# A list scheduler's cost table, replaced by measured instruction spacings, in a Mamba and attention kernel

## The chip, the cores and the metric

The kernel runs on one core of a Trainium2 chip. The metric is the device time of one execution in microseconds (us). A core has five engines that work side by side, each through its own queue in order: PE (TensorE, matrix products), DVE (VectorE), ACT (ScalarE, which also loads a function table when the kind of function changes), POOL (GpSimd) and SP, which here issues the DMA transfers.

## The reference

Two layers are applied to an image batch x of shape (2, 256, 64, 64), float32; each image is 256 channels by 4096 positions.

```python
# layer 0: Mamba, along the 4096 positions of each image
y = group_norm(x);  yn = layer_norm(y) * gamma + beta
xm, z = split(yn @ W_in.T)                      # 512 channels each
u = silu(conv1d(xm, conv_w, 4 taps) + conv_b)
dt, B, C = split(u @ W_xp.T)                    # 16, 16, 16
dt = softplus(dt @ W_dt.T + b_dt)
h[t] = exp(dt[t] * A) * h[t-1] + (dt[t] * u[t]) * B[t]    # state 512 x 16
ym = (sum_n h[t] * C[t] + u * D) * silu(z)
y2 = ym @ W_out.T + yn
x = x + gelu(y2 @ W1.T + b1) @ W2.T + b2 + y2
# layer 1: attention with 8 heads of 32 channels over the 4096 positions
q, k, v = qkv_w @ group_norm(x) + qkv_b
x = x + softmax(q^T k / sqrt(32)) v
```

## The kernel before

The program has two stages, one after the other: `mamba_stage` and `attention`.

**Tiles and steps.** The Mamba stage goes through 16 tiles: 2 images of 8 tiles, each of 512 positions. A tile has four blocks of 128 channels (KD = 4), and the 16 states of each channel are laid out so that four of them share the 128 partitions with 32 channels. This gives 32 steps per tile (STEPS), 512 in all. One step (`step`, from L809) does, for two rows of 128 x 512:

- two decays `da = exp(dt * A)` on ACT (L828)
- one matmul on PE that spreads a row of B over the partitions into `bn`, in PSUM (L444 with `pick`)
- two products `dbu = dtu * B`: one on DVE into `bn` (L834), and one that is on POOL in three steps of four and on DVE in the fourth (also L834)
- two scans on DVE (L839), which are the recurrence along the positions
- a copy of the last state on ACT (L842), `keep`, needed by the next tile
- the product of h with C on POOL, in place, 128 x 1024 (L845), which therefore waits for `keep`
- after every second step, four matmuls on PE that add up over the states into `y` (L871); with the last of a block, DVE multiplies y with the gate z (L881)

**Around the steps.** `front` prepares a tile before its steps start: normalisation, the projection and convolution of each block (`conv`, with SiLU), and `softplus`, whose three POOL products of 128 x 512 are L614, L615 and L617. `gate` makes silu(z). `back` comes after the steps of a tile: W_out (L641), the residual sum (L652), the up-projection with GELU (L666), the down-projection (L675, L677), the final sum (L687) and statistics (L688). `qkv` makes the first image's q, k and v for the attention while the second image's tiles run, so that the second half of the stage has this on top. It evacuates each block on ACT (L730) and DVE (L734) and stores it by DMA (L739, L759). `back` and `qkv` take turns with one buffer `hid` of 8 x 512. dt and dtu go through DRAM: stored at L608, and loaded again in the layout of the steps at L792; rows of B and C are loaded at L804.

**What sets the order.** The order of the Mamba stage isn't written by hand. Each piece of work is added to a `Plan` by `add(engine, due, cost, emit, reads, writes, tables, lands)`: the engine, a due time counted in steps, a cost in us, and what it reads and writes. `Plan.order` then plays the program through once, when the kernel is built: whenever an engine is free, it takes from the ready tasks the one that is due first. A task that needs another function table on ACT ranks SWITCH = 6 steps later, and none more than HORIZON = 24 steps past the oldest open one is taken. The engine is then held for the task's cost (1.3 us more for a table load), and what depends on it counts as ready 0.2 us after its end (HANDOVER), plus `lands` for a DMA. Buffers come from rings with a fixed number of places, and a task without a place waits. The result is one order of instructions for each engine, fixed in the program. On the chip, an engine works through its queue in that order, whatever the planned times were. Costs thus take no time themselves. They only shape the order, and with it the places of the table loads.

The attention stage is emitted in a hand-made order after it: per 128 keys the logits on PE (L1131), exponentials on ACT (L1144), values on PE (L1161), and sums on DVE (L1153, L1191) and POOL (L1185 to L1194).

Of the kernel before, what the change touches and what calls it, by code (L numbers as in the profile page):

```python
# [13 lines left out]
AF = mybir.ActivationFunctionType  # L14
# [5 lines left out]
P = 128  # L20
# [238 lines left out]
def mamba_stage(ctx, tc, xs, stats_out, consts, w, outs, scratch):  # L259
# [13 lines left out]
    nc = tc.nc  # L273
    ident, gmat, lnmat, eps_t = consts
    IMAGES = len(xs)
# [213 lines left out]
    def front(i):  # L489
# [12 lines left out]
        for k in range(KC):  # L502
            add("ACT", due - 41, 0.75, lambda k=k: norm(k), [yn[k], scales_buf[b * KC + k]], [yn[k]])


        mean = Buf(mm)
        add("PE", due - 40, 1.8, lambda: matmul(mean.tile, [(lnmat, yn.tile[:, k, :]) for k in range(KC)]), [yn], [mean])
        sq = [Buf(r_tmp) for _ in range(KC)]
        var = Buf(mm)
        for k in range(KC):  # L510

            def centre(k=k):
                nc.vector.tensor_sub(yn.tile[:, k, :], yn.tile[:, k, :], mean.tile)

            add("DVE", due - 39, 0.7, centre, [mean], [yn[k]])
            square = lambda k=k: nc.scalar.activation(sq[k].tile, yn.tile[:, k, :], AF.Square)
            add("ACT", due - 38, 0.65, square, [yn[k]], [sq[k], var] if k == 0 else [sq[k]])

# [4 lines left out]

        add("PE", due - 37, 1.9, lambda: matmul(var.tile, [(lnmat, s.tile) for s in sq]), sq, [var])
        add("ACT", due - 36, 1.25, rstd, [], [var], ("exp",))
        for k in range(KC):

            def scale(k=k):
                y = yn.tile[:, k, :]
                nc.vector.scalar_tensor_tensor(y, y, gamma[:, k : k + 1], var.tile, ALU.mult, ALU.mult)  # L530

            def shift(k=k):
                y = yn.tile[:, k, :]
                nc.scalar.activation(y, y, AF.Identity, bias=beta[:, k : k + 1])  # L534

            add("DVE", due - 35, 0.75, scale, [var], [yn[k]])
            add("ACT", due - 34, 0.75, shift, [], [yn[k]])
        d.u = [Buf(r_u) for _ in range(KD)]
# [17 lines left out]

        add("PE", due - 14, 3.6, project, d.u, [pp, proj, bc])
        add("ACT", due - 13, 0.6, lambda: nc.scalar.copy(proj.tile[:NP, :], pp.tile[:NP, :]), [pp], [proj])
        add("ACT", due - 13, 0.6, lambda: nc.scalar.copy(bc.tile, pp.tile[:NP, :]), [pp], [bc])
        add("SP", due - 12, 0.4, store_bc, [bc], [d.bc], lands=1.6)  # L560
        add("DVE", due - 12, 0.7, halves, [pp, proj], [proj])
        d.dt, d.dtu = [None] * KD, [None] * KD
# [3 lines left out]
    def conv(d, b, k, due):  # L566

        px, pc, xm = Buf(mm), Buf(mm), Buf(r_xm, 2)
        h = halo_buf[b * KD + k]

        def project():
            matmul(px.tile, [(w_in[:, c, bass.ts(k, P)], d.yn.tile[:, c, :]) for c in range(KC)])

        def convolve():
            matmul(pc.tile, [(taps[:, k, j, :], xm.tile[:, j : j + T]) for j in range(TAPS)])

        def silu():
            nc.scalar.activation(d.u[k].tile, pc.tile, AF.Silu, bias=conv_b[:, k : k + 1])

        add("PE", due, 1.8, project, [d.yn], [px, xm])  # L580
        add("POOL", due, 0.2, lambda: nc.gpsimd.tensor_copy(xm.tile[:, 0:HALO], halo[:, b, k, :]), [h], [xm[0]])
        add("ACT", due + 1, 0.6, lambda: nc.scalar.copy(xm.tile[:, HALO:], px.tile), [px], [xm[1]])
        add("POOL", due + 2, 0.2, lambda: nc.gpsimd.tensor_copy(halo[:, b, k, :], xm.tile[:, T:]), [xm], [h])
        add("PE", due + 2, 3.6, convolve, [xm], [pc, d.u[k]])
        add("ACT", due + 4, 0.6, silu, [pc], [d.u[k]], ("silu",))

    def softplus(d, k, due):
# [21 lines left out]

        add("PE", due, 0.8, lambda: matmul(pd.tile, [(w_dt[:, i, bass.ts(k, P)], d.proj.tile) for i in range(2)]), [d.proj], [pd, dt, lw])  # L610
        add("ACT", due + 1, 1.95, exps, [], [pd, dt], ("exp",))
        add("ACT", due + 1, 1.2, logs, [pd], [lw, w1], ("exp",))
        add("DVE", due + 2, 0.7, rest, [pd], [w1])
        add("POOL", due + 3, 1.27, lambda: nc.gpsimd.tensor_sub(lw.tile, lw.tile, w1.tile), [w1], [lw])  # L614
        add("POOL", due + 3, 1.27, lambda: nc.gpsimd.tensor_add(dt.tile, dt.tile, lw.tile), [lw], [dt])  # L615
        add("SP", due + 3.5, 0.9, lambda: store(d.dt[k], dt, "dt_dram"), [dt], [d.dt[k]], lands=2.0)
        add("POOL", due + 3.5, 1.27, lambda: nc.gpsimd.tensor_mul(lw.tile, dt.tile, d.u[k].tile), [dt, d.u[k]], [lw])  # L617
        add("SP", due + 4, 0.9, lambda: store(d.dtu[k], lw, "dtu_dram"), [lw], [d.dtu[k]], lands=2.0)

    def gate(d, k, due):  # L620

        pz, z = Buf(mm), Buf(r_z)
        d.z.append(z)

        def project():
            matmul(pz.tile, [(w_in[:, c, bass.ds(DI + k * P, P)], d.yn.tile[:, c, :]) for c in range(KC)])

        add("PE", due, 1.8, project, [d.yn], [pz, z])
        add("ACT", due + 1, 0.6, lambda: nc.scalar.activation(z.tile, pz.tile, AF.Silu), [pz], [z], ("silu",))

    def back(i):
# [5 lines left out]
        for m in range(KC):  # L637
# [7 lines left out]
            for k in range(0, KD, 2):  # L645
                reads = d.z if k == 0 else d.z[k : k + 2]
                add("PE", due + 2 * m, 1.9, lambda k=k, project=project: (project(k), project(k + 1)), reads, [po])
            add(
                "DVE",
                due + 2 * m + 1,  # L650
                0.7,
                lambda m=m, po=po: nc.vector.tensor_add(yn.tile[:, m, :], yn.tile[:, m, :], po.tile),  # L652
# [6 lines left out]
        for f in range(KH):  # L659
# [7 lines left out]

            add("PE", due + 5 + 1.5 * f, 1.9, up, [yn], [ph, hid if f == 0 else hid[f]])
            add("ACT", due + 6 + 1.5 * f, 0.7, gelu, [ph], [hid[f]], ("gelu",))
        for m in range(KC):  # L670
# [10 lines left out]
            for f in range(0, KH, 2):  # L681
                reads = [hid, yn[m]] if f == 0 else [hid[f], hid[f + 1]]
                add("PE", due + 19 + 4 * m + f / 2, 2.7 if f == 0 else 1.8, lambda f=f, down=down: down(f), reads, [acc])

# [4 lines left out]

            add("DVE", due + 24 + 4 * m, 1.45, end, [acc], [xt[m], stats_bufs[IMAGES + b][m * NT + t]])  # L690
        store = lambda: nc.sync.dma_start(image_tile(outs[b], t), xt.tile)
        add("SP", due + 29, 1.7, store, [xt], [stored[b * NT + t]], lands=3.3)

    def qkv(b, t, due):
# [25 lines left out]
        for k in range(KC):  # L720
            add("ACT", due + 2, 0.75, lambda k=k: norm(k), [hid[3 + k], scales_buf[(IMAGES + b) * KC + k]], [hid[3 + k]])
        for n, (i, m) in enumerate(((1, 0), (1, 1), (0, 0), (0, 1))):
# [20 lines left out]
            at = due + 3 + 2.2 * n  # L743
            add("PE", at, 1.8, project, [hid[k] for k in range(5)], [pm, *halves])
            add("ACT", at + 0.5, 0.7, high, [pm], [hid[5]])
            add("DVE", at + 1, 0.7, low, [pm, hid[5]], [hid[6]])
            add("SP", at + 1.5, 1.7, store, halves, [], lands=3.3)
        for j in range(0, T // P, 2):
# [15 lines left out]
            at = due + 4 + 2.2 * j  # L764
            add("PE", at, 1.8, project, [hid[k] for k in range(5)], [pv, hid[7]])
            add("ACT", at + 0.5, 0.7, lambda pv=pv: nc.scalar.copy(hid.tile[:, 7, :], pv.tile), [pv], [hid[7]])
            add("SP", at + 1, 1.0, store, [hid[7]], [], lands=2.5)
# [41 lines left out]
    def step(g):  # L809
# [37 lines left out]
        for j in range(2):  # L847
            add("ACT", g - 6 + j, 0.71, lambda j=j: decay(j), [dt[j]], [da[j]], ("exp",))
        add("PE", g - 6, 0.4, broadcast_b, [d.proj], [bn])
        if pooled(g):  # L850
            add("POOL", g - 6, 1.27, lambda: times_b(nc.gpsimd, dbu1, 1, rows_b), [dtu[1], rows_b], [dbu1])
        else:
            add("DVE", g, 0.7, lambda: times_b(nc.vector, dbu1, 1, bn), [dtu[1], bn], [dbu1])
        add("DVE", g, 0.7, lambda: times_b(nc.vector, bn, 0, bn), [dtu[0]], [bn])
        for j, dbu in ((1, dbu1), (0, bn)):
            add("DVE", g, 1.27, lambda j=j: scan(j), [da[j], dbu, state_buf[states[j]]], [h[j]])
        add("ACT", g - 6, 0.25, keep, [h], [state_buf[at] for at in states])
        add("POOL", g - 4, 2.36, times_c, [rows_c], [h])
        if quarter == 0:
# [18 lines left out]

        add("PE", g - 3, 1.9 if qd == 0 else 1.1, add_up, [s.h for s in pair] + ([d.u[k]] if qd == 0 else []), [y])
        if qd == NQ - 1:  # L880
            add("DVE", g + 2.5, 0.7, lambda: nc.vector.tensor_mul(d.z[k].tile, y.tile, d.z[k].tile), [y], [d.z[k]])  # L881

# [578 lines left out]
```

## Time and profile before

| what | value |
|---|---|
| median of 3 runs | 4506.31 us (4498.84 to 4507.30) |
| profiled execution: span from first to last instruction | 4505.2 us |
| granted TensorE clock, mean | 0.977 |
| busy over the span: PE, DVE, ACT, POOL | 94%, 86%, 84%, 85% |
| last y x z product of the Mamba stage (L881) | 2066.8 us after the start |
| first logits of the attention (L1131) | 2115.5 us |
| ACT table loads at L244 | 332, of 1283 ns each |

The page doesn't list a time of its own for the profiled execution; its span is 1.1 us below the median of the runs.

Durations of the instructions that matter below, as means: C product on POOL (L845) 2371 ns, dbu on POOL (L834) 1283, the scans (L839) 1273 and 1264, bn on DVE (L834) 681, decay (L828) 701, state copy (L842) 189, bn matmul 595, GELU (L666) 686. The C products and the dbu products on POOL have 512 and 384 instructions.

How to read it: in a row of the timeline stand the start, the duration, the engine and line, and in brackets how long the engine had been idle before and which instruction ended that. In a table by stretch, each engine has its busy time and in brackets the number of instructions. Instructions that follow each other closely on one engine overlap a little, so that the sum of their durations is more than the time they occupy together. The spacing, from one start to the next, is the smaller number.

### The profile page before, as it was taken

To read this page: it belongs to the slowest core of one execution; us is meant where nothing else is said; L and a number is where in the kernel's file an instruction comes from. 1 tells how busy PE (TensorE), PEld (TensorE's weight loads), DVE (VectorE), ACT (ScalarE), POOL (GpSimd) and SP (SyncE) were. 2 spreads that over 40 slices of the span, in tenths; PEclk is the share of its full clock that TensorE was granted. 3 is DMA by queue.
4 is the path that set the end of the run, shared out by engine and by line. 5 is a ranking of instruction groups with operands and counts; after the bars stand their busy time and mean duration, and the time that the engine had idled before them with its cause. 6 is when DMAs were issued, how large, how long until landed. Compare 5 with 4: busy or idle time off the path is not lost.

```text
span 4505.2 us, 53942 instructions
## 1 busy us (share of the span) xinstructions
PE 4257.1 (94%) x18530; PEld 1642.2 (36%) x18530; DVE 3890.9 (86%) x3309; ACT 3768.4 (84%) x4842; POOL 3807.4 (85%) x2249
## 2 busy tenths in 40 slices
PE   5789999999999999988999999999999999999998
PEld 2233333333333333333333333333353333333333
DVE  4999999999999989894888888888848888888888
ACT  4788888888788889873999999999849999999997
POOL 2999999999999999994788888888728888888886
PEclk8899999999999999999999999999999999999999
DMA  5233333333443434445210140101091110401100
GB/s 192 94 120 101 110 125 122 127 127 127 143 148 134 139 126 140 147 153 144 58 27 17 29 101 17 26 17 30 24 265 35 46 26 17 101 17 29 27 19 8
DMA packets 172281, 389.23 MB, mean 86 GB/s; under 512 B 23392, under 2 KB 49760, under 8 KB 163808
## 3 DMA queue, kind: packets, MB, share of 16 engines
q1 hardware_dynamic: 171120, 383.37, 27.4%
q8 instruction: 147, 2.41, 0.2%
q10 hardware_dynamic: 880, 2.36, 0.2%
q14 instruction: 134, 1.10, 0.1%
HBM read 292.33 MB, written 93.32 MB: 86 GB/s over the span
## 4 chain that ended last, share of the span: by engine, by line
PE 57%; DVE 4%; ACT 3%; POOL 3%; issue 2%; DMA 1%; DVEq 0%; POOLq 0%; SPq 0%; ACTq 0%
PE s L1131 25%; PE po L1161 24%; PE mm L444 3%; DVE h L839 2%; POOL h L845 2%; ACT da L828 1%; ACT L244 1%; PE mm L677 1%; PE s L1016 1%; PE y L871 1%; POOL dbu L834 1%; PE sums_ps L1212 1%; DVE bn L834 1%; PE mm L641 0%; PE bn L444 0%
## 5 line engine op out<-in xcount | busy, mean ns | idle before, releaser
L1153 DVE TENSOR_REDUCE chunk<-chunk 128x1024 f32<-128x4096 f32 x288 | 1270.6, 4412 | 242.4 <-ACT chunk L1144 242.3
L1194 POOL TENSOR_TENSOR acc_p<-acc_p,e 128x1024 f32<-128x1024 f32 x480 | 1151.9, 2400 | 196.7 <-ACT e L1144 178.0
L1144 ACT ACTIVATE chunk<-s 128x1024 f32<-128x1024 f32 x992 | 1121.5, 1131 | 185.5 <-PE s L1131 139.9
L845 POOL TENSOR_TENSOR h<-h,c 128x1024 f32<-128x1024 f32 x512 | 1208.5, 2371 | 42.0 <-ACT state L842 28.9
L1131 PE MATMUL s<-q,k 128*128 128x512 f32 x4096 | 1228.4, 422 | 5.8 <-ACT chunk L1144 4.9
L1161 PE MATMUL po<-chunk,v 128*32 128x512 f32 x3968 | 1121.7, 642 | 0.0
L1161 PE MATMUL po<-e,v 128*32 128x512 f32 x4224 | 1080.0, 605 | 0.0
L1144 ACT ACTIVATE e<-s 128x1024 f32<-128x1024 f32 x1056 | 1072.7, 1019 | 7.4 <-PE s L1131 6.9
L1131 PEld LDWEIGHTS s<-q,k 128*128 128x128 f32 x4096 | 691.3, 188 | 1014.4 <-issue 915.0
L828 ACT ACTIVATE da<-dt_rep,neg_a 128x512 f32<-128x512 f32 x1024 | 690.5, 701 | 128.7 <-DVE h L839 106.0
L1192 POOL TENSOR_TENSOR acc_p<-acc_p,e 128x512 f32<-128x512 f32 x480 | 620.2, 1292 | 129.3 <-ACT e L1144 106.6
L839 DVE TENSOR_TENSOR_SCAN h<-da,state,dbu 128x512 f32<-128x512 f32 x512 | 650.5, 1273 | 42.8 <-POOL dbu L834 40.2
L839 DVE TENSOR_TENSOR_SCAN h<-da,state,bn 128x512 f32<-128x512 f32 x512 | 647.1, 1264 | 11.6
L834 POOL TENSOR_TENSOR dbu<-dtu_rep,b 128x512 f32<-128x512 f32 x384 | 488.5, 1283 | 19.7 <-DMA dtu_rep<-dtu_dram 15.0
L244 ACT ACT_TABLE_LOAD x332 | 426.0, 1283 | 6.7 <-PEq L1451 0.7
L444 PE MATMUL bn<-proj,pick 112*128 112x512 f32 x512 | 296.4, 595 | 112.2 <-DVE h L839 111.6
L871 PE MATMUL y<-h,sum 128*32 128x512 f32 x2048 | 359.1, 635 | 42.2 <-POOL h L845 42.1
L834 DVE TENSOR_TENSOR bn<-dtu_rep,bn 128x512 f32<-128x512 f32 x512 | 348.6, 681 | 41.4 <-PE bn L444 27.8
L1191 DVE TENSOR_TENSOR acc<-acc,e 128x512 f32<-128x512 f32 x448 | 310.7, 694 | 30.9 <-ACT e L1144 17.5
L1161 PEld LDWEIGHTS po<-chunk,v 128*32 128x32 f32 x3968 | 144.3, 108 | 361.5 <-issue 349.9
L444 PE MATMUL mm<-yn,w_in 128*128 128x512 f32 x512 | 254.7, 625 | 10.3 <-ACT yn L534 9.1
L444 PE MATMUL mm<-yn,w 128*128 128x512 f32 x512 | 246.5, 611 | 4.2 <-ACT hid L666 2.1
(143 smaller groups left out, 4016.3 us busy)
## 6 DMA issues: line engine op xcount, KB each, us to landing
dt_rep<-dt_dram SPq DMA_DIRECT2D x128, 512.0 KB, 5.1
dtu_rep<-dtu_dram SPq DMA_DIRECT2D x128, 512.0 KB, 5.7
k<-qk_dram SPq DMA_DIRECT2D x62, 512.0 KB, 7.3
q<-qk_dram SPq DMA_DIRECT2D x124, 256.0 KB, 4.7
b<-bc_dram SPq DMA_DIRECT2D x64, 256.0 KB, 3.0
c<-bc_dram SPq DMA_DIRECT2D x64, 256.0 KB, 3.7
dt_dram<-dt SPq DMA_DIRECT2D x64, 256.0 KB, 2.0
dtu_dram<-lw SPq DMA_DIRECT2D x64, 256.0 KB, 2.3
```

The source lines that it names most:

```text
L244: self.nc.scalar.preload_act_table_set(self.TABLES[task.table])
L444: nc.tensor.matmul(out, lhsT=lhsT, rhs=rhs, start=(i == 0), stop=(i == len(pairs) - 1))
L828: nc.scalar.activation(da[j].tile, dt.tile[:, j, :], AF.Exp, scale=scale)
L834: engine.tensor_mul(out.tile, dtu.tile[:, j, :], rows.tile)
L839: nc.vector.tensor_tensor_scan(h.tile[:, j, :], da[j].tile, dbu.tile, initial, ALU.mult, ALU.add)
L845: nc.gpsimd.tensor_tensor(h.tile, h.tile, rows_c.tile.unsqueeze(1).to_broadcast([P, 2, T]), ALU.mult)
L1131: nc.tensor.matmul(ps[:, j, :], lhsT=keys[i // NT, kt][:, h, kj : kj + P], rhs=queries[i][:, h, :], start=True, stop=True)
L1144: nc.scalar.activation(e, todo[s].s[half], AF.Exp, scale=SCALE)
L1153: nc.vector.tensor_reduce(out, terms, AX.XY, ALU.add)
L1161: nc.tensor.matmul(tiles[i].po[h * D : (h + 1) * D, :], lhsT=v[:, c, g * P + h * D : g * P + (h + 1) * D], rhs=todo[s].e[h // 2][:, h % 2, :],
L1192: nc.gpsimd.tensor_add(acc_p[:, 1, :], acc_p[:, 1, :], eb[:, 1, :])
L1194: nc.gpsimd.tensor_add(acc_p, acc_p, eb)
```

## The change

Only the third argument of `add`, the cost, is changed, in the functions of the Mamba stage. Costs of SP's tasks, of some tiny ones, the due times, the landings, HANDOVER, TABLE, SWITCH, HORIZON and the rings stay. The core of the diff (each line pair cut to its cost):

```diff
# front
-norm 0.75   mean, var (PE) 1.8, 1.9    centre 0.7   square 0.65   rstd 1.25   scale, shift 0.75, 0.75
+norm 0.72   mean, var (PE) 1.72, 1.72  centre 0.6   square 0.52   rstd 1.19   scale, shift 0.66, 0.62
-project (PE) 3.6    proj and bc copies (ACT) 0.6, 0.6     halves (DVE) 0.7
+project (PE) 3.44   proj and bc copies (ACT) 0.48, 0.48   halves (DVE) 0.72
# conv
-add("PE", due, 1.8, project, [d.yn], [px, xm])
+add("PE", due, 1.72, project, [d.yn], [px, xm])
-xm copy (ACT) 0.6    convolve (PE) 3.6    silu (ACT) 0.6
+xm copy (ACT) 0.49   convolve (PE) 3.44   silu (ACT) 0.59
# softplus
-PE 0.8   exps 1.95   logs 1.2    rest (DVE) 0.7    three POOL products 1.27 each
+PE 0.5   exps 1.76   logs 0.97   rest (DVE) 0.58   three POOL products 1.23 each
# gate
-PE 1.8    silu 0.6
+PE 1.72   silu 0.5
# back
-W_out pair 1.9    sum (DVE) 0.7   up 1.9    gelu 0.7    down 2.7, then 1.8     end (DVE) 1.45
+W_out pair 1.72   sum (DVE) 0.6   up 1.72   gelu 0.59   down 2.58, then 1.72   end (DVE) 1.37
# qkv
-norm 0.75   project 1.8    high (ACT) 0.7    low (DVE) 0.7    v project 1.8    v copy (ACT) 0.7
+norm 0.71   project 1.72   high (ACT) 0.59   low (DVE) 0.66   v project 1.72   v copy (ACT) 0.49
# step
-            add("ACT", g - 6 + j, 0.71, lambda j=j: decay(j), [dt[j]], [da[j]], ("exp",))
-        add("PE", g - 6, 0.4, broadcast_b, [d.proj], [bn])
+            add("ACT", g - 6 + j, 0.63, lambda j=j: decay(j), [dt[j]], [da[j]], ("exp",))
+        add("PE", g - 6, 0.26, broadcast_b, [d.proj], [bn])
-dbu on POOL 1.27   dbu and bn on DVE 0.7, 0.7
+dbu on POOL 1.23   dbu and bn on DVE 0.6, 0.6
-            add("DVE", g, 1.27, lambda j=j: scan(j), [da[j], dbu, state_buf[states[j]]], [h[j]])
-        add("ACT", g - 6, 0.25, keep, [h], [state_buf[at] for at in states])
-        add("POOL", g - 4, 2.36, times_c, [rows_c], [h])
+            add("DVE", g, 1.185, lambda j=j: scan(j), [da[j], dbu, state_buf[states[j]]], [h[j]])
+        add("ACT", g - 6, 0.1, keep, [h], [state_buf[at] for at in states])
+        add("POOL", g - 4, 2.32, times_c, [rows_c], [h])
-add_up (PE) 1.9 with the block's first, else 1.1    y times z (DVE) 0.7
+add_up (PE) 1.92 with the block's first, else 1.06   y times z (DVE) 0.58
```

The program that comes out has the same arithmetic and the same instructions in another order on every engine, save for the table loads on ACT, which follow the order.

## The prediction

> **What bounds the kernel now.** First the page's engine shares and the rows by slice; the first half of the span is the Mamba stage, the second the attention, whose order is written out by hand and which the change does not touch.
>
> ```profile
> PE 4257.1 (94%) x18530; PEld 1642.2 (36%) x18530; DVE 3890.9 (86%) x3309; ACT 3768.4 (84%) x4842; POOL 3807.4 (85%) x2249
> ...
> DVE  4999999999999989894888888888848888888888
> ACT  4788888888788889873999999999849999999997
> POOL 2999999999999999994788888888728888888886
> ```
>
> The averages mislead: in the Mamba slices POOL is at 9 throughout, which its 85% of the whole span hides. So next the busy times by stretch. I cut at 106 us (POOL is running the steps), at 1180 (the second image's tiles, with the first image's QKV work beside them, have begun) and at 2064, where POOL's last step ends.
>
> ```profile
> 106.00:1180.00 1074.00, 973.53 (x2938) 359.70 (x2936) 1000.36 (x1087) 885.86 (x1465) 1060.89 (x674) 0.95 0.34 114
> 1180.00:2064.00 884.00, 823.88 (x2561) 323.95 (x2559) 812.76 (x893) 720.59 (x1196) 838.83 (x523) 0.97 0.42 143
> ```
>
> The last busy time is POOL's: idle 1074.0 - 1060.9 = 13.1 us in the first stretch and 884.0 - 838.8 = 45.2 in the second. The tile's end (its last product with z, L881, four per tile) comes every 120.8 us for tiles 4 to 8, and for tiles 9 to 15 every (1947.2 - 1069.8) / 7 = 125.3 us. POOL's own work per tile is 32 products with C and 36 of half size: 32 x 2.32 + 36 x 1.23 + some 1.5 of small copies = 120.1 us, with the spacings that two back-to-back products show (4.7 us a pair at L845, 2.52 at L834). **So the first half already stands at POOL's floor, and the second lies about 4.5 us per tile above it.** POOL's waits say why:
>
> ```profile
> POOL h L845 <- ACT state L842: 28.2, 34, 2.7
> POOL dbu L834 <- DMA dtu_rep<-dtu_dram: 8.2, 7, 2.0
> POOL h L845 <- issue: 5.6, 2, 4.4
> POOL dbu L834 <- DVE h L839: 4.6, 2, 3.1
> ```
>
> The largest is that the product with C overwrites h, and so waits until ACT has copied the last state out of it (L842). One such place in time, ACT's queue first and POOL's second:
>
> ```profile
> 1269.45 1.28 ACT L244 ACT_TABLE_LOAD   x1
> 1270.75 0.69 ACT L578 ACTIVATE u<-mm,conv_b 128x512 f32<-128x512 f32 x1
> 1271.33 0.19 ACT L842 COPY state<-h 128x2 f32<-128x2 f32 x1
> ```
> ```profile
> 1271.65 2.36 POOL L845 TENSOR_TENSOR h<-h,c 128x1024 f32<-128x1024 f32 x1 [2.74 <-ACT state L842]
> ```
>
> A copy of 0.19 us stood behind a table load and a SiLU, and POOL lost 2.74 us. Last, the stage's end: after POOL has ended (2064.8), QKV's and the MLP's rest for the last tile runs alone until the first attention matmul at 2115.5.
>
> ```profile
> 2069.49 0.69 ACT L730 ACTIVATE hid<-mm,b_qkv 128x512 fp32r<-128x512 f32 x1 [7.17 <-PE mm L444]
> ...
> 2078.03 0.69 ACT L730 ACTIVATE hid<-mm,b_qkv 128x512 fp32r<-128x512 f32 x1 [6.24 <-PE mm L444]
> ...
> 2083.12 0.69 ACT L730 ACTIVATE hid<-mm,b_qkv 128x512 fp32r<-128x512 f32 x1 [4.40 <-DMA qk_dram<-hid]
> ...
> 2087.97 0.69 ACT L666 ACTIVATE hid<-mm,b 128x512 f32<-128x512 f32 x1 [2.85 <-DMA qk_dram<-hid]
> ```
>
> Each QKV block waits for the one before to be stored, and the GELUs wait for the last, because all use the one hid buffer.
>
> **What the Trainium skill says.** "Perfetto Trace Analysis", Identifying the Most-Contended Engine, takes occupancy as the measure for Vector, Scalar and GpSimd but not for matmuls; here it picks POOL (98.8% of the first stretch), although PE shows 93% in the second. "Trainium Architecture — The Big Picture", Inside one NeuronCore: each engine has its own instruction stream and they meet only through semaphores; the 2.74 us above agree: an order that is bad for ACT is paid on POOL. "ScalarE: Activation LUTs", What ACT_TABLE_LOAD costs, gives 1283 ns per load plus a drain of about 1380 ns, and an overlap of about 93 ns between ACTIVATEs. The trace agrees on the load (1283) but not on the drain: the SiLU started 1.30 us after the load did. Its decays last 701 ns each, and four took 2.52 us, so they are 0.63 us apart: an overlap of 0.07, the difference between a duration and a spacing.
>
> **The change, part by part.** No instruction's work changes; the planner's sums and thereby the order do.
>
> (a) Planned work per tile, from the code's costs. Before: DVE 122.8, POOL 122.8, ACT 113, PE 112 us; with QKV's share in the second half DVE 125.6, ACT 119, PE 123. After: DVE 112, POOL 120.1, ACT 100, PE 101; with QKV 114, 120.1, 105, 112. The old plan held four engines for equally full in the second half; the new one sees what the trace shows (DVE 812.8 / 884 x 125.3 = 115 busy). It should place QKV and MLP work where there is room. Ceiling: POOL's 45.2 us idle there, 58.3 with the first stretch.
>
> (b) Are the new costs too short? A result is planned as ready at cost + 0.2. A scan: 1.185 + 0.2 = 1.385, while the trace has it read 1.29 us after its start; C product 2.52 against 2.37 + 0.03; decay 0.83 against 0.70; state copy 0.30 against 0.22. All still cover the duration. Only the single matmul for bn does not: 0.26 + 0.2 = 0.46 against a duration of 0.595. DVE already waits 27.8 + 20.9 us on it at L834. Bounds: nothing, where DVE has other slack (it is idle 9%), and at most 0.15 us x 512 = 77 on DVE if each were met; on POOL's path I take 0 to 5 us.
>
> (c) Order, read from the built programs engine by engine. Loads of dtu_rep: SP's costs are unchanged, but its order follows what it waits for. In tiles 12 to 16 the shortest lead of a load before its first use, counted in POOL work, was 2.3 us and becomes 4.6 to 4.8, against 5.7 us from issue to landing: most of the DMA waits (8.2 us) go. But two things get worse. The distance on POOL from making dbu to the C product of the same step, which covers two scans and the state copy, falls from 7.6 to about 6.1 us in the first half and from about 8.3 to 6.3 in the second. And table loads in the stage rise from 331 to 353, those planned between a step's second scan and its state copy from 12 to about 16 a tile. Behind such a load on ACT stand the copy and the decays, and POOL waits. 22 x 1.283 = 28 us more on ACT, which is idle 18%: at nothing if its slack covers them, 28 if POOL waited for each.
>
> Sum for the second half: of 45 us idle I let about a third go, 2 us for each of 7.3 tiles: -15. First half: it stands at the floor and can only lose; less distance costs perhaps 0.5 us in each of eight tiles: +4. The ramp until 75 us keeps its order: 0.
>
> (d) The end. Before, after the last y the third QKV block came behind 12 matmuls of W_out: its evacuation started 78.03 - 66.76 = 11.3 us after that y, the GELUs 21.2 after. In the new order only one pair of W_out stands ahead of it, and the second block has moved ahead of the last y, where PE was idle 2.7 us. Then: 1.72 + 1.72 + 0.2 = 3.6 to the evacuation, 5.1 to the store's landing (2078.03 to 2083.12), 4.8 for the next: 13.5. GELUs start 7 us sooner, and W_out and the first three up-projections (8.6 + 5.2 = 13.8) are then late as well, so no more. -7.
>
> Sum: -15 + 4 - 7 = **-18 us**. The profiled execution's span is 4505.2, 1.1 below the median of 4506.3; from the median: 4488.
>
> **Rivals.** *Ceiling reached*: all POOL idle of the second half and the tail go: 4506 - 45 - 7 = 4454. For: the new plan has POOL alone as bound; against: (c), and DMA and PE clock (0.97) still vary. *Nothing seen*: POOL's idle moves to other places, tail and first half cancel: 4502. For: POOL stood behind the same copies in both orders. *Slower*: tighter distances and more table loads put POOL behind the state copy in all tiles. Needed from dbu's end: two scans 2.45, copy and handovers 0.25, a running DVE instruction 0.6 to 1.2, a table load with its function 2.0: 5.3 to 5.9 us, and with dbu's own 1.23, 6.5 to 7.1, more than the new mean of 6.1 to 6.3, less than the old 7.6. If that costs 2 us in each of 16 tiles, +32 - 7 = +25: 4531. It decides from some 0.5 us per tile on, where it has eaten the tail. Against: the planner models these waits too. *The change doesn't do what it says*: the costs do agree with the spacings (b), so I give this no share of its own.
>
> **Numbers.** Forecast (4476 to 4497) 0.47; ceiling 0.14; nothing seen 0.22; slower 0.17. Range 4462 to 4520: it leaves out half of the ceiling's cases and the worse part of the slower ones. A measurement can tell about 0.2%, 9 us: faster 0.61, same 0.22, slower 0.17.
>
> **What would show it.** Right: tiles 9 to 15 at about 123 us, tiles 4 to 8 at 121 to 121.5, fewer DMA waits on POOL, first GELU of the last tile some 14 us after the last y. Wrong: tiles 4 to 8 above 122, or POOL's wait for the state copy grown above 40 us. The attention must stay at about 2390 us.

## The result and the profile after

The changed kernel took 4499.66 us (median of 12 runs, 4492.70 to 4506.44) against 4506.28 (12 runs, 4498.44 to 4510.28) for the kernel before: a ratio of 0.999, 95% interval 0.9982 to 0.9997. That is 6.6 us less, a third of the 18 us that were forecast, and inside the 0.2% that a measurement can tell from no change. The profiled execution has a span of 4500.3 us, 4.9 less than before.

The page's shares and slices, in the order of the prediction's fence:

```profile
PE 4230.6 (94%) x18530; PEld 1635.6 (36%) x18530; DVE 3895.3 (87%) x3309; ACT 3791.8 (84%) x4864; POOL 3808.7 (85%) x2249
...
DVE  4899999999999999995888888888848888888887
ACT  4688888888889898884999999999849999999997
POOL 2999999999999999994888888888728888888886
```

They hide the change, since the work is nearly the same. ACT has 22 instructions more, the table loads (354 for 332). So the time is taken from the ends of tiles (the start of every fourth y x z product, L881), which cut the span into pieces that add up:

| us | before | after | difference | forecast |
|---|---|---|---|---|
| start to end of tile 1 | 219.2 | 225.4 | +6.2 | 0 to 75 us |
| tiles 2 to 8 | 850.6 | 864.1 | +13.5 | +4 with tile 1's steps |
| tiles 9 to 16 | 997.0 | 979.4 | -17.6 | -15 |
| end of tile 16 to the first logits | 48.7 | 41.6 | -7.1 | -7 |
| attention, to the end of the span | 2389.7 | 2389.8 | +0.1 | 0 |

**The whole error is in the first half.** The busy times by stretch, cut at tile 1's end, tile 8's end and tile 16's end, first of before, then of after (PE, PEld, DVE, ACT, POOL with the numbers of instructions, then clock, DMA share and GB/s):

```profile
219.19:1069.80 850.61, 779.67 (x2360) 291.06 (x2358) 792.17 (x862) 708.21 (x1166) 840.51 (x534) 0.96 0.35 118
1069.80:2066.81 997.01, 929.58 (x2884) 364.38 (x2884) 915.64 (x1007) 811.36 (x1344) 947.90 (x592) 0.97 0.41 139
```
```profile
225.41:1089.49 864.08, 782.49 (x2372) 292.23 (x2371) 792.36 (x860) 717.42 (x1175) 840.09 (x533) 0.96 0.34 116
1089.49:2068.89 979.40, 909.71 (x2891) 362.08 (x2890) 918.98 (x1007) 829.83 (x1362) 947.37 (x592) 0.98 0.41 141
```

POOL does the same work, 840 and 948 us. Its idle time goes from 850.6 - 840.5 = 10.1 to 24.0 us in the first row and from 49.1 to 32.0 in the second: +13.9 and -17.1, which is the difference in the table to half a microsecond. That alone doesn't show that POOL is the bound, since any engine with unchanged work shows it (DVE's idle time in the first row goes from 58.4 to 71.7 us). What does is that before the change POOL was idle for only 1.2% of the first row. (Of tile 1's 6.2 us, 3.8 are idle POOL time, all after 75 us; in the other 2.4 POOL did more work, which belongs to the next tile.) What POOL waited for in the first of the two stretches before the change, with the longest row alone:

```profile
POOL h L845 <- ACT state L842: 6.8, 8, 2.0
```

And after it, in both stretches:

```profile
POOL h L845 <- ACT state L842: 19.4, 25, 1.4
POOL dbu L834 <- POOL h L845: 0.9, 1, 0.9
POOL dbu L834 <- DMA dtu_rep<-dtu_dram: 0.4, 1, 0.4
```
```profile
POOL h L845 <- ACT state L842: 22.1, 33, 2.6
POOL h L845 <- issue: 3.1, 1, 3.1
```

In the first half the wait for the state copy was 6.8 us in 8 places and is now 19.4 in 25. In the second half that wait stays (20.6 before), and the DMA waits of 8.2 us have gone, as forecast. Between 106 us and tile 8's end I took each of these waits apart, with the step's own two scans, copy and C product, which the order of the built program gives. Of 22.3 us after the change, in 30 places, 9.1 passed with both scans done and the copy standing behind other work on ACT, 5.3 before the later scan had ended, and 7.9 with the copy itself and the handovers, some 0.27 in each place. Before, it was 5.3, nothing and 2.3, in 9 places. So both the queue on ACT and late scans have grown. A place with all three parts, in ACT's queue, DVE's and then POOL's:

```profile
277.12 1.28 ACT L244 ACT_TABLE_LOAD   x1
278.41 0.69 ACT L578 ACTIVATE u<-mm,conv_b 128x512 f32<-128x512 f32 x1
279.00 0.59 ACT L629 ACTIVATE z<-mm 128x512 f32<-128x512 f32 x1
279.48 0.19 ACT L842 COPY state<-h 128x2 f32<-128x2 f32 x1
```
```profile
277.90 2.45 DVE L839 TENSOR_TENSOR_SCAN h<-da,state,dbu 128x512 f32<-128x512 f32 x2
```
```profile
279.75 2.36 POOL L845 TENSOR_TENSOR h<-h,c 128x1024 f32<-128x1024 f32 x1 [1.44 <-ACT state L842]
```

POOL was free from 278.31. The step's later scan is the first of the two in DVE's row and ended at 279.17, 0.86 us later. The copy then stood 0.31 us behind the second SiLU, which a table load and another SiLU had preceded, and the copy with its handovers took the last 0.27 of the 1.44 us. The stage's end, in the rows of ACT that answer to those shown before:

```profile
2072.51 0.69 ACT L730 ACTIVATE hid<-mm,b_qkv 128x512 fp32r<-128x512 f32 x1 [5.72 <-PE mm L444]
...
2079.38 0.69 ACT L730 ACTIVATE hid<-mm,b_qkv 128x512 fp32r<-128x512 f32 x1 [6.18 <-PE mm L444]
...
2084.59 0.69 ACT L666 ACTIVATE hid<-mm,b 128x512 f32<-128x512 f32 x1 [3.23 <-PE mm L444]
```

The third QKV block is evacuated 3.6 us after tile 16's end (2068.89), where it was 11.2 before, and the first GELU runs 15.7 us after it for 21.2.

### The profile page after: what moved, and what is told of

Read it like the earlier page. It is cut to its first block, busy times and chain, and to the rows that moved or that the text cites. A ratio compares the mean times of both kernels' runs of the same rounds, so it can differ in the third digit from the quotient of the medians.

```text
span 4500.3 us, 53959 instructions
## 1 busy us (share of the span) xinstructions
PE 4230.6 (94%) x18530; PEld 1635.6 (36%) x18530; DVE 3895.3 (87%) x3309; ACT 3791.8 (84%) x4864; POOL 3808.7 (85%) x2249
## 4 chain that ended last, share of the span: by engine, by line
PE 67%; DVE 9%; POOL 8%; ACT 7%; issue 6%; DMA 2%; SPq 0%; DVEq 0%; POOLq 0%; ACTq 0%
PE s L1131 25%; PE po L1161 24%; PE mm L444 9%; DVE h L839 5%; POOL h L845 4%; ACT L244 3%; ACT da L828 2%; PE y L871 2%; POOL dbu L834 2%; DVE bn L834 2%; PE mm L641 2%; PE bn L444 1%; PE s L1016 1%; DMA dtu_rep<-dtu_dram 1%; PE mm L677 1%
## 5 line engine op out<-in xcount | busy, mean ns | idle before, releaser
L871 PE MATMUL y<-h,sum 128*32 128x512 f32 x2048 | 330.8, 639 | 19.6 <-POOL h L845 19.5
L1191 DVE TENSOR_TENSOR acc<-acc,e 128x512 f32<-128x512 f32 x448 | 310.6, 693 | 30.7 <-ACT e L1144 17.2
```

## The experiments

All kernels start from one form in which each changed cost is written as a pair, old and new, for example `add("PE", g - 6, (0.4, 0.26), ...)`, and one rule in `Plan.add` picks from it. With the rule `cost = new` the order is that of the changed kernel on every engine, with `cost = old` that of the kernel before.

```diff
     def add(self, engine, due, cost, emit, reads=(), writes=(), tables=(), lands=0.0):
+        old, new = cost if isinstance(cost, tuple) else (cost, cost)
+        cost = new        # the rule; each experiment has its own
```

The theories at the start: A, the planner sees room on ACT and puts table switches ahead of the state copies; B, results are planned as ready too early. The rivals that were formed on the way stand in the expectations. The measured pieces of all runs are in one table at the end of this section. Ratios are against runs of the kernel before on the same chip.

**e1: old costs in the first half, new in the second**

```diff
+        cost = old if self.early else new
...
     for i, d in enumerate(tiles):
+        plan.early = i < NT
```

> The work added while the first image's tiles are planned (tiles 1 to 8, with the next tile's front) keeps the old costs, that of the second image's tiles gets the new ones. If gain and loss belong to their halves, tile 8 ends near 1070 us as before the change, tiles 9 to 16 take about 979 us as after it, and the rest some 42: about 4481 us in all (span 4480). If the two halves hang together, so that a new order in the second half only pays after a new order in the first, tiles 9 to 16 stay near 990 to 997 and the total at 4492 to 4499.

4489.76 us, ratio 0.997 (0.996 to 0.9981), where the changed kernel has 0.999 (0.9982 to 0.9997): faster than both. Tile 8 ends at 1071.7 and the end takes 41.5, as expected. Tiles 9 to 16 take 989.0 instead of 979: the ninth tile, the first after the change of costs, has 131.4 us. So the first half keeps its floor, but the second keeps only 8.0 of its gain of 17.6 us, which lies between the two expectations.

**e2, e3, e4: ACT's costs old; readiness by the old costs; DVE's costs old**

```diff
+        cost = old if engine == "ACT" else new     # e2
...
+        cost = old if engine == "DVE" else new     # e4
...
+        cost = new                                 # e3
+        late = old - new
...
-                done = end + task.lands
+                done = end + task.late + task.lands
```

> New costs on all engines but ACT, which keeps the old ones (table loads planned in the stage fall from 353 to about 315). Theory A, room on ACT: the loss of the first half comes from table switches and short functions that the planner puts ahead of the state copies because it sees room on ACT; then tile 8 ends back near 1070 to 1075 us and POOL's wait for the state copy in the first half falls from 22 to about 8 us. Theory B, readiness: the loss comes from results being planned as ready earlier on all engines, DVE's scans above all; then the first half stays above 1080. The time would be about 4482 by A, 4495 to 4500 by B.

> An engine is planned as held for the new cost, but what depends on a task counts as ready only after the old, longer one. Theory B, readiness: this gives back the distance between dbu and the C product, so the first half returns to tile 8 at 1070 to 1075 us, and the second half keeps its gain (about 979): near 4482. Theory A, room on ACT: it does not help, since engines are still planned as freer than before: tile 8 at 1085 to 1090, about 4500.

> New costs on all engines but DVE, which keeps the old ones: scans 1.27, products 0.7. By theory B most of the first half's loss goes, since the scans are planned as ready later again: tile 8 near 1072, about 4484. By theory A nothing much changes in the first half (1085 to 1090), and the second loses what DVE's room gave: 4500 to 4510.

4549.20 (1.0102), 4519.67 (1.0038) and 4517.04 us (1.0031): all three are slower than either whole set of costs, and none brings the first half back to its floor (861.0, 863.2 and 859.6 us for tiles 2 to 8). **Neither theory is the whole cause.** Fewer table loads (316 in e2) bring POOL's wait for the state copy in tiles 2 to 8 down to 14.6 us, not to 8, and readiness alone leaves it at 21.6 (e3). In e4 that wait is back at 5.4 us, as B would have it, but POOL is still idle for 16.7, and 7.5 of this has no releaser in the profile: the loss came back in another form. What the three show besides is in the second half: 1014.6, 999.7 and 1004.0 us, worse than all old.

**e5, e6: a nudge that says nothing of the chip**

```diff
-    HANDOVER = 0.2
+    HANDOVER = 0.21
```

> All costs old, and HANDOVER 0.21 instead of 0.2: a nudge of 0.01 us that says nothing new of the chip. Theory C, sensitivity: the order is decided by near ties, and the old order's first half at the floor (120.8 us per tile, every tile alike) is one draw among many; then the nudge alone moves tile 8's end from 1070 to somewhere in 1075 to 1090, and the total by 5 us or more, most likely up, to about 4515. If the old order is good because its costs leave slack, the nudge changes little: tile 8 at 1068 to 1073, total within 3 us of the kernel before.

> All costs new, and HANDOVER 0.21. Theory C: the total moves by 5 us or more against 4499.7, either way, and tiles 9 to 16 leave 979 by more than 5. If what the change brought is due to its costs, the first half stays at 1085 to 1092, tiles 9 to 16 at 976 to 983, the end at 42: 4497 to 4503.

4510.25 us (1.0014, 1.0007 to 1.0021) with the old costs, and 4511.73 (1.0015, 1.0008 to 1.0021) with the new ones, where the kernel before and the changed one take 4504 to 4506 and 4500. So 0.01 us in the planner moves the one kernel by some 6 us and the other by 11 to 12, as much as the whole change. Each stays within 0.2% of the kernel before, with an interval that leaves out no change. In the profile of e5, tiles 2 to 8 take 854.8 us for 850.6. The profiled execution of e6 was a short one, its span some 9 us below what its median suggests, so its pieces can't show where its 12 us lie.

**e7: table switches put off**

```diff
-SWITCH = 6
+SWITCH = 8
```

> All costs new, and SWITCH 8 instead of 6: the planner puts a change of function table off for longer; the program has 11 table loads fewer than with the change alone. Theory A, room on ACT: state copies stand less often behind table loads, so POOL's idle in the first half falls from 28 us towards 20 and the total to about 4490. By theory C the number of table loads decides nothing, and the total is a draw between 4485 and 4520.

4503.66 us (0.9999, 0.9991 to 1.0008), with 343 table loads for 354. POOL's idle in tiles 1 to 8, from 106 us on, falls from 28.1 to 22.7, 5.4 of the 8 us that A expected, and the second half gives it back (986.4). It doesn't decide between A and C.

**e8: only DVE's costs new**

> Only DVE's costs new, all others old: the complement of the run in which only DVE's were old, which took 4517 against 4499.7 with all new. If the parts of the change add up, DVE's part is worth 4499.7 - 4517.0 = -17, and this kernel takes about 4504 - 17 = 4487. If parts don't add up (theory C, or theory D: a plan pays only when all its costs agree with each other), it is above 4500; by D above the kernel before, as the other mixtures were, at 4510 to 4550.

4520.55 us (1.0039). The parts don't add up: DVE's costs are worth -17 with all others new and +16 with all others old. The costs of one engine pay only beside those of the others (theory D).

**e9, e10: proportion or margin**

```diff
+        cost = new if old == new else 1.03 * new     # e9
...
+        cost = old if old == new else 0.97 * old     # e10
```

> Every changed cost is 1.03 times its new value: the new proportions between engines, with some of the old margin over the chip. Theory M, margin: the old costs kept POOL at its floor in the first half because everything on the chip was somewhat quicker than planned; then tile 8 ends at 1070 to 1076, tiles 9 to 16 take 980 to 989, and the total is about 4488. Theory P, proportions: what counts is which engine is planned as fullest; then this kernel belongs to the new family, tile 8 at 1082 to 1090, 4498 to 4508.

> Every changed cost is 0.97 times its old value: the old proportions with less margin. By theory P this belongs to the old family: tile 8 ends at 1069 to 1076, tiles 9 to 16 take 993 to 999, the end 48 to 51, total 4503 to 4512. By theory M the first half goes up to 1080 or more and the total to 4512 to 4520.

4521.81 (1.0037) and 4499.64 us (0.9987, 0.9979 to 0.9996). Neither theory holds: margin on the new costs does not bring the first half back (865.6), and less of it on the old ones gives 858.4 there, 990.6 in the second half and 41.6 at the end: much what the change does, and to the same total. So the change's net gain needs no measured costs. In the first half the wait for the state copy is only 5.0 us here, of 18.0 in which POOL is idle, as in e4.

**e11, e12: PE's costs old; POOL's costs old**

```diff
+        cost = old if engine == "PE" else new        # e11
...
+        cost = old if engine == "POOL" else new      # e12
```

> New costs on all engines but PE, which keeps the old ones. PE is the one engine whose new costs are below what the trace shows: at a clock of 0.96 in the first half, and with 0.26 for the bn matmul that lasts 0.595. If that is what makes DVE late in the first half, tile 8 ends at 1072 to 1078, and the total is 4487 to 4493. Theory D (a plan pays only when its costs agree with each other) has it above 4505, as the mixtures with ACT or DVE old.

> New costs on all engines but POOL, which keeps 2.36 and 1.27 for 2.32 and 1.23. POOL is the bound of the first half, and its new cost takes 2.7 us per tile out of the plan, in which the others have to fit. If the lost margin on POOL makes the first half's loss, tile 8 ends at 1070 to 1076 and the total is about 4487. If not, it is within the new family: tile 8 at 1082 to 1090, 4496 to 4508.

4529.92 (1.005) and 4555.06 us (1.0102). POOL's margin isn't it. But e11 finds the first half: after tile 2, every tile takes 120.8 to 121.1 us, POOL's floor, with DVE, ACT and POOL at their new costs. Its busy times for tiles 2 to 8, what POOL waited for there, and DVE for bn (the lines of the code are two further down):

```profile
225.48:1074.81 849.33, 773.18 (x2369) 285.06 (x2367) 791.47 (x861) 721.24 (x1179) 840.16 (x533) 0.98 0.36 119
```
```profile
POOL h L847 <- ACT state L844: 5.8, 10, 1.2
```
```profile
DVE bn L836 <- PE bn L446: 12.3, 7, 3.5
...
DVE dbu L836 <- PE bn L446: 2.6, 2, 1.3
```

POOL's idle is 849.3 - 840.2 = 9.1 us for 24.0 with the whole change, and DVE's wait for bn is 14.9 us. The same rows before the change and after the whole of it:

```profile
DVE bn L834 <- PE bn L444: 13.9, 13, 1.6
...
DVE dbu L834 <- PE bn L444: 2.6, 7, 0.5
```
```profile
DVE bn L834 <- PE bn L444: 28.3, 19, 4.1
...
DVE dbu L834 <- PE bn L444: 1.3, 3, 0.6
```

The price is paid later: tiles 9 to 16 take 1012.7, and the end 49.0.

**e13, e14, e15: only PE's costs new; bn's cost old; PE's costs old but for bn**

```diff
+        cost = new if engine == "PE" else old                               # e13
...
+        cost = 0.4 if cost == (0.4, 0.26) else new                          # e14
...
+        cost = old if engine == "PE" and cost != (0.4, 0.26) else new       # e15
```

> Only PE's costs new, all others old: the complement of the run with PE old. Theory E, PE's new costs alone make the first half's loss and the end's gain: tiles 2 to 8 take 858 us or more instead of 850.6, with DVE waiting more than 25 us for bn in them, and the end takes about 42 us instead of 48.7. Theory D (agreement): the first half is no worse than in other mixtures, and the end is not bound to PE.

> All costs new but that of the bn matmul, which keeps 0.4 for 0.26 (it lasts 0.595). If the understated bn is what makes DVE late in the first half, tiles 2 to 8 take 849 to 853 us as with PE all old, the second half stays near 979 to 989 and the end at 42: about 4485. If it is PE's other costs, tiles 2 to 8 stay at 858 to 865.

> All costs new but PE's, which are old save for bn at 0.26: the other half of PE's part. If the understated bn makes the loss, tiles 2 to 8 take 858 or more; if PE's other costs do, they take 849 to 853.

4523.29 (1.0042), 4503.94 (0.9998, 0.999 to 1.0007) and 4519.62 us (1.0037). With PE's costs alone, the first half loses more than with the whole change (876.1), the end gains (42.8), and the second half gains nothing (996.1). Tile 2 takes 138.8 of the 876.1 us; tiles 3 to 8 take 737.3, where they took 726.5 before and 738.8 after the whole change. So PE's costs are enough for the loss and for the end, not for the second half. Within PE either part is enough to lose the floor: with bn back at 0.4 tiles 2 to 8 take 859.6, with all of PE but bn back 866.5, which is 17.2 us more than in e11 for bn's cost alone. Only when the whole of PE is old are they at the floor.

**e16, e17, e18: PE's costs old at first, new later; with a nudge; the change of costs a tile earlier**

```diff
+        cost = old if self.early and engine == "PE" else new
...
+        plan.early = i < NT          # e16; e17 with HANDOVER = 0.21 also
...
+        plan.early = i < NT - 1      # e18
```

> PE's costs old while the first image's tiles are planned, new from then on; all other engines new throughout. If each half's result goes with the PE costs in force, tiles 2 to 8 take 849 to 851, tiles 9 to 16 979 to 992 with one slow tile at the change of costs, and the end 42: 4484 to 4496, faster than both kernels. If not, the second half is at 1000 or more and the total above 4505.

> PE's costs old while the first image's tiles are planned, else all new, and HANDOVER 0.21: the nudge that moved both whole kernels. If PE's costs really set the first half, tiles 2 to 8 take 849 to 855 us again; tiles 9 to 16 stay in the new family, 979 to 989; the end 42; total 4485 to 4497. If the kernel without the nudge was a lucky draw, tiles 2 to 8 take 858 or more and the total is above 4500.

> PE's costs change one tile earlier, after seven tiles instead of eight. If the slow tile (131.8 us, the ninth) belongs to the change of costs, the eighth becomes slow and the ninth takes about 123. If it belongs to the start of QKV, which comes with the ninth tile in any kernel (125.9 before, 128.7 after), the ninth stays at 128 to 132 and the total at 4485 to 4497.

4491.05 (0.9971, 0.996 to 0.9983), 4493.55 (0.9977, 0.9966 to 0.9987) and 4489.45 us (0.9963, 0.995 to 0.9977): all faster than the kernel before, and with medians below the changed one's, though the intervals of e16 and e17 touch its interval (0.9982 to 0.9997). The nudge leaves the first half where it is, 850.2 for 849.5. But it hardly changed the order there: in the built programs of e16 and e17, 20 of PE's first 726 tasks and 36 of DVE's first 1001 stand in another place, where the nudge of e6 moved 297 and 344. So e17 doesn't settle whether e16's first half was a lucky draw. In e18 the eighth tile takes 120.6 us and the ninth still 129.1, so the slow ninth tile belongs to QKV's start and not to the change of costs. Tiles 2 to 8 and 9 to 16 of e18:

```profile
225.44:1075.51 850.07, 774.50 (x2370) 285.99 (x2368) 792.57 (x860) 720.54 (x1178) 840.34 (x533) 0.98 0.35 118
```
```profile
1075.51:2053.61 978.10, 910.68 (x2894) 361.97 (x2892) 919.03 (x1007) 830.03 (x1362) 947.65 (x592) 0.98 0.42 141
```

**All runs, by their profiles.** "PE" says which costs PE had while the first image's tiles were planned. The profiled execution of e15 was some 7 us longer than its median suggests, and those of e6 and e18 some 9 and 6 shorter, so single pieces are good to several us. The six first halves at the floor (before, e1, e11, e16, e17, e18), though, agree within 1.6. They are two orders and not six: up to the last tile of the half, the built program of e1 has the order of the kernel before, and those of e16, e18 and nearly e17 have that of e11.

| run | PE, first half | tile 1 | tiles 2-8 | tiles 9-16 | end | median |
|---|---|---|---|---|---|---|
| before | old | 219.2 | 850.6 | 997.0 | 48.7 | 4506.3 |
| after | new | 225.4 | 864.1 | 979.4 | 41.6 | 4499.7 |
| e1 halves | old | 220.8 | 850.9 | 989.0 | 41.5 | 4489.8 |
| e2 ACT old | new | 221.2 | 861.0 | 1014.6 | 63.1 | 4549.2 |
| e3 ready by old | new | 224.3 | 863.2 | 999.7 | 41.4 | 4519.7 |
| e4 DVE old | new | 220.0 | 859.6 | 1004.0 | 42.5 | 4517.0 |
| e5 old, 0.21 | old | 219.5 | 854.8 | 995.1 | 49.4 | 4510.3 |
| e6 new, 0.21 | new | 224.7 | 858.8 | 988.9 | 42.0 | 4511.7 |
| e7 SWITCH 8 | new | 223.8 | 859.1 | 986.4 | 41.5 | 4503.7 |
| e8 DVE new | old | 225.8 | 853.6 | 1004.3 | 50.9 | 4520.6 |
| e9 new x 1.03 | x 1.03 | 226.4 | 865.6 | 994.5 | 41.8 | 4521.8 |
| e10 old x 0.97 | x 0.97 | 217.6 | 858.4 | 990.6 | 41.6 | 4499.6 |
| e11 PE old | old | 225.5 | 849.3 | 1012.7 | 49.0 | 4529.9 |
| e12 POOL old | new | 230.2 | 884.5 | 1010.4 | 42.2 | 4555.1 |
| e13 PE new | new | 217.6 | 876.1 | 996.1 | 42.8 | 4523.3 |
| e14 bn old | new but bn | 225.9 | 859.6 | 980.8 | 44.8 | 4503.9 |
| e15 PE old but bn | old but bn | 226.7 | 866.5 | 997.1 | 44.5 | 4519.6 |
| e16 PE old early | old | 226.7 | 849.5 | 986.8 | 41.6 | 4491.1 |
| e17 the same, 0.21 | old | 225.4 | 850.2 | 985.0 | 41.5 | 4493.6 |
| e18 a tile earlier | old | 225.4 | 850.1 | 978.1 | 41.6 | 4489.5 |

In tiles 2 to 8 the runs with all of PE old have 849.3 to 854.8 us, those without 858.4 to 884.5, whatever the other engines' costs. In tiles 9 to 16 the runs with every engine new there (bn, HANDOVER and SWITCH apart) have 978.1 to 989.0. The others, the kernel before among them, have 990.6 to 1014.6. The step between the groups is 3.6 us in the first half and 1.6 in the second, less than a single piece is good to, so that the extremes of the groups say more than their edges.

## Why the prediction was right or wrong

- **What bounds the stage**: right for the first half, where POOL was idle for 1.2% of tiles 2 to 8, and no kernel here went below 849 us for them. In the second half POOL was the fullest engine too, but with PE and DVE close to it (947.9, 929.6 and 915.6 us of 997.0).
- **(a), second half, -15**: -17.6. Right in size. The reason given, that the plan now sees room where there is room, is too simple. With one engine left at its old costs the second half is no better than before (1004.0, 1010.4, 1012.7, 1014.6 for DVE, POOL, PE and ACT old). Beside the new costs it took all four, though the old ones times 0.97 also gained 6.4 (990.6). e11 fits the working there: PE was then planned at 123 us per tile beside POOL's 120.1, as the fullest engine, which it isn't.
- **(c), loads of dtu_rep**: right. The 8.2 us of waits for them in the second half have gone from the list.
- **(d), the end, -7**: -7.1, right in the mechanism, and lucky in the sum. The third block came 3.6 us after the last tile instead of 11, as worked out. The fourth then stood behind twelve matmuls of W_out and came 6.9 us after the third, not 5.1, so that the GELUs started 5.5 us sooner rather than 7. The rest came from the up-projections, which ran with less waiting (8.85 us for the last 20 matmuls, 10.51 before); nobody had forecast that. With the other costs all old or all new, PE's costs make this part: it is there with only PE new (42.8) and gone with only PE old (49.0). But e10 has it with scaled costs (41.6), and with ACT's costs old the end is the longest of all (63.1).
- **(c), first half, "0.5 us in each of eight tiles: +4"**: this is the step that failed. The waits named are the ones that came, but they are priced at a quarter: POOL's idle grew by 13.9 us in seven tiles, 2.0 each, and tile 1 ended 6.2 us later, all of it after the ramp. The text had the better number itself: its slower rival worked out that 6.5 to 7.1 us are needed where the new order leaves about 6.1 on average, priced that at 2 us per tile, and set it aside because "the planner models these waits too". In the first half that price was about right. In the second it wasn't: the wait for the copies rose only from 20.6 to 22.1 us.
- **(b), the new costs**: right that bn is too short, and wrong to value that at 0 to 5 us on POOL's path and to look no further on PE. bn's cost alone made 17.2 us in tiles 2 to 8 (e15 beside e11). A smaller slip has no weight in the sum: four decays in 2.52 us are three spacings and one duration, so they are 0.61 us apart and not 0.63, and overlap by 0.09. PE's costs decide the first half: all old, they give tiles 2 to 8 849.3 to 854.8 us in four different orders (before, e5, e8, e11), beside old and new costs on the others; with some or all of them changed, twelve orders give 858.4 to 884.5.
- **Why PE's costs do this** is argued only. The clock of PE doesn't explain it. Its mean in these tiles is 0.96, but it is full or half: after the change 917 spacings between matmuls of 128 x 512 fall into full clock, with a median of 0.43 us, so that the four matmuls of a pair of products take the planned 1.72, and 41 fall into short stretches at half clock, with 0.85. The mean was also 0.96 before, at the floor, and e15 plans its pairs at the old 1.8 and is 17 us off. What agrees is that DVE, which needs bn for each step, waits longer for it: 29.6 us in tiles 2 to 8 after the change, 16.5 before. Of these, 21.3 and 7.7 us came where PE went into bn's matmul straight from other work in its queue, without a wait for another engine that the profile shows; in e11 it is 6.6. But e8 has 16.4 of these with 853.6 us, and e4 and e14 have short waits for bn in all (14.7 and 18.3) with the first half still 9 us above the floor. So this isn't the whole cause, and what else is stays open.
- **The signs of being wrong** both came: tiles 4 to 8 took 123.5 us each, above 122, and POOL's wait for the state copy grew from 28.2 to 44.4 us in the stage, above 40. Tiles 9 to 15, at 123.8, and the attention were as forecast.
- **Rival "the change doesn't do what it says"**: it was given no share. e10 shows that it deserved one. The old costs, merely times 0.97, give 4499.6 us, the changed kernel's time, with no measured spacing in them. And e6 shows that the changed kernel's gain doesn't stand a nudge of 0.01 us. In this kernel's profile the second half and the end do gain. That measured costs by themselves bring a better order isn't shown.

## What to carry to other kernels

When an order comes from a list scheduler, judge a change to its costs stage by stage against the floor of the fullest engine: a stage that stands at its floor can only lose, and should keep the costs that put it there (here 4489 to 4494 us in the four kernels that did so, e1 and e16 to e18). Look at the costs of the engines that feed the bound one as well, PE's here. Which cost is the better one isn't settled by measuring it: PE's old costs were the better ones in the first half, and all the old ones times 0.97 did as well as the measured ones. And nudge a constant that means nothing before a few microseconds are put down to a reason: here 0.01 us of HANDOVER moved one kernel by 6 us, another by 11 to 12, and a third (e17 beside e16) by 2 to 3.

## What the runs showed that was not expected

One engine's costs can be worth more than the whole change: POOL's 0.04 us per instruction, put back alone (e12), cost 55 us. All of it came as waiting, since no instruction's work changed. And one program's executions spread by up to 15 us (4502.4 to 4517.2 in e6), so that a single profile's total says little about a change of this size, while its pieces at a floor repeat within 1.6 us.
